# A graph block and a transformer block in one kernel: norm rows spread over slots, wider ranges for projections, modulation in other steps

## The chip, the cores and the metric

The kernel runs on one core of a Trainium2 chip. The metric is the device time of one execution in microseconds (us). Five engines work side by side, each through its own queue of instructions in order: TensorE (PE in the profile) multiplies matrices and transposes, VectorE (DVE) and ScalarE (ACT) work on rows and can read PE's results, GpSimd (POOL) works on rows in SBUF, and SyncE (SP) issues the DMA transfers. They wait for each other by semaphores. All data is float32; a product of two float32 tiles shows as two matmul records in the trace.

## What is computed

Input x has 4 batch elements of 1024 tokens of 512 features; there is one condition vector of 512 features per element. Two blocks follow each other:

```python
# block 0: graph attention; each node looks at 20 nodes, 16 heads, two directions d
self_feat = concat(v, q) @ W_self.T + b_self
for d in range(2):
    aff = einsum(qh, kh) / sqrt(32)            # qh, kh: projections of self_feat
    w = softmax(where(cond > 0, aff, NEG) + label_bias)
    output += einsum(einsum(w, kv), Wout[d]) + bout[d]
x = v + relu(output)

# block 1: conditioned transformer, 16 heads of 64, MLP of 2048
mod = silu(c) @ W_mod + b_mod
sh_msa, sc_msa, g_msa, sh_mlp, sc_mlp, g_mlp = split(mod, 6)
x = x + g_msa * attention(layernorm(x) * (1 + sc_msa) + sh_msa, W_qkv, W_out, b_out)
x = x + g_mlp * (gelu(h @ W1 + b1) @ W2 + b2)  # h: layernorm(x) * (1 + sc_mlp) + sh_mlp
```

## The kernel before

The 4096 tokens are 32 tiles of 128 rows. The program is one long sequence written out by hand; each engine executes its part of it in the order in which the Python code calls the functions. There are three stages.

**Graph attention** is the loop `for s in range(-4, NTA + 2)`. In step s the tiles s-1 to s+4 are at different stations of a pipeline: transposes of x (`g_xT`), the self features (`g_self`), scores (`g_scores`, matmuls of line 643), softmax, weights, output rows to DRAM (`x1d`). One PSUM bank, tag "tr", is shared by the transposes of x and of the features, by the transposes of the norm (`norm_T`) and by the modulation (`g_mod`). `g_modload(r)` loads a quarter of W_mod and `g_mod(r)` multiplies it with silu(c); r = 0 and 1 give shift and scale, r = 2 and 3 the gates, which DVE reads from the bank in line 753. The buffer of the loads holds one quarter. In this stage the first batch element is also normalized: `norm_load(0, k)` loads four tiles, `norm_rows(0, k)` subtracts the mean and multiplies by 1/std, a row of tiles at a time, and `norm_T(0, k, c)` transposes 128 features of the four tiles and applies shift and scale into `hT`.

**Attention** has 4 x 8 x 8 = 256 slots: batch element b, pair of heads gp, query tile t. A slot s consists of a fixed part and of fill. In the fixed part PE makes the scores of two heads into the two "sc" tiles (line 960), DVE takes their maxima (`largest`, line 971), ACT the exponentials (`weights`, line 977), which frees the score tiles for the next slot; ACT scales the first head's weights and GpSimd the second's (`scaled`, line 986). DVE transposes the weights of the slot before in blocks of 32 (`turn`, line 995), the first head's ahead of this slot's maxima and the second's behind them, and after each second slot SP moves them into wT by eight DMAs (line 999).

The fill is a list. `add(lo, hi, units, place, f, *args)` says that f may go into any slot from lo to hi and weighs `units` on PE. A planner puts everything at lo first and then moves pieces to the emptiest slot of their range until nothing gets better. Within a slot, fill runs after the fixed part, by `place`: loads (0), attention times v (1), projections (2), transposes of the norm (3), work of DVE, ACT and GpSimd (4). The pieces that matter here:

- `mm_qk(b, gp, k, n, half, bank)`: half of the sum for q (k = 0) or k (k = 1) of a pair of heads and of half n of the tokens, 1 unit; 8 per pair. It needs `hT` of half n. `mm_v` is the same for v, one tile of tokens each.
- `attend` (line 922), `project` (line 940, whose rows DVE adds into `xr` in line 948).
- norm pieces with times `ld`, `rw`, `tr` relative to `at`, the first slot of the batch element.
- Tiles of PSUM for all of these come from one group "mm" of four banks. `xl`, the rows to be normalized, has four buffers, so that a second `norm_load` waits for the transposes of the first; `hT` has two.

Before slot 256 the fill also holds the first seven products of the **MLP** (`first`, from the function `seven`, in slots NS-6 to NS-1, with NS = 256). They need `mlp_rows` and `mlp_weights`, sums that GpSimd makes (lines 431 to 441). Two of the products start with an opening matmul (line 466) that reads `hT`, which `mlp_rows` also writes. The rest of the MLP follows after the slots and isn't touched.

Of the kernel before, what the change touches and what calls it, by code (L numbers as in the profile page):

```python
# [12 lines left out]
F32 = mybir.dt.float32  # L13
I32 = mybir.dt.int32
AF = mybir.ActivationFunctionType
ALU = mybir.AluOpType
# [3 lines left out]
P = 128  # L20
S = 1024
# [20 lines left out]
def cond_block_kernel(  # L42
# [26 lines left out]
    nc = tc.nc  # L69
# [60 lines left out]
    with ExitStack() as gctx:  # L130
        KC0 = GH * 2 * NG // P
        HF = GH * NG
        gp = gctx.enter_context(tc.tile_pool(name="gp", bufs=1))
# [13 lines left out]
        with ExitStack() as sctx:  # L147
# [69 lines left out]
            for h in range(2):  # L217
                pt = sps.tile([P, FC, P], F32, name="pt", tag="s")
                for c in range(FC):
                    k = h * FC + c  # L220
# [43 lines left out]
            for d in range(2):  # L264
# [19 lines left out]
                v = sp.tile([KV, F], F32, name="vrow", tag="vrow", bufs=2)  # L284
# [59 lines left out]
        VB = 4  # L344
# [3 lines left out]
        def norm_load(st, k):  # L348
            for i in range(k * VB, (k + 1) * VB):
                t = rp.tile([P, F], F32, name="xl", tag="xl", bufs=VB)  # L350
                nc.sync.dma_start(t, NORM[st][0][i])
                xl[st, i] = t

        def norm_rows(st, k):
            _, mv, rs, _, _ = NORM[st]
            for i in range(k * VB, (k + 1) * VB):
                nc.vector.tensor_scalar(
                    xl[st, i], xl[st, i], mv[:, i, 0:1], rs[:, i : i + 1], ALU.subtract, ALU.mult
                )

        def norm_T(st, k, c, bank, on_act=True):

# [33 lines left out]

        def mm_qk(b, gp, k, n, half, bank):

            if half == 0:
                if n == 0:  # L400
                    (qT, kT)[k][b, gp] = qp.tile([P, S], F32, name="qk"[k] + "T", tag="qk"[k] + "T", bufs=2)
                part["qk"] = bank("pqk")
            pt = part["qk"]
            for c in (2 * half, 2 * half + 1):
                nc.tensor.matmul(  # L405
                    pt,
                    lhsT=wqk[b, gp][:, c, k, :],
                    rhs=hT[0, 2 * b + n][:, c, :],
                    start=(c == 0),
                    stop=(c == FC - 1),  # L410
                )
            if half == 1:
                if k == 0:
                    nc.scalar.mul(qT[b, gp][:, n * F : (n + 1) * F], pt, float(D**-0.5))
                else:
                    o = kT[b, gp].rearrange("p (c m k) -> p m k c", c=4, m=NT)
                    nc.scalar.copy(o[:, n * 4 : n * 4 + 4], pt.rearrange("p (m k c) -> p m k c", c=4, k=32))
# [371 lines left out]
        for s in range(-4, NTA + 2):  # L789
            if s == -4:  # L790
                for i in range(5):
                    g_load(i)
            else:
                do(g_load, s + 4)
            if s in (1, 7, 13, 19):
                g_modload(s // 6)
            do(g_scores, s)
            if s == NTA:
                ahead(4)
            do(g_weightsT, s - 1)  # L800
            do(g_soft1, s)
            do(g_startscores, s + 1)
            do(g_xT, s + 3)
            do(g_startattend, s - 1)
            do(g_soft2, s)
            do(g_mask2, s + 2)
            do(g_mask1, s + 3)
            do(g_soft3, s)
            do(g_self, s + 2)
            if s >= NTA - 2:  # L810
                ahead((2, 1, 1, 0)[s - NTA + 2])
            do(g_selfT, s + 1)
            do(g_soft4, s)
            if 0 <= s - 2 < NTA:
                statistics(xs.pop(s - 2), mv1[:, s - 2, :], wp)
            do(g_soft5, s)
            do(g_attend, s - 1)
            do(g_selfout, s + 2)
            do(g_rows, s - 1)
            do(g_start, s + 3)  # L820
            do(g_sum, s + 4)

            if s in (6, 12, 18, 24):
                g_mod(s // 6 - 1)
            if s == 12:
                rstd(rs1, mv1, 0, NT)
            if s in (14, 21):
                norm_load(0, s // 7 - 2)
            if s in (16, 23):
                norm_rows(0, s // 7 - 2)  # L830
            if s in (17, 18, 19, 20, 24, 25, 26, 27):
                norm_T(0, s // 24, (s - 17) % 7, bank_l0)
            if s == 25:
                load_qk(0, 0)
                load_v(0, 0)
                load_qk(0, 1)
                load_v(0, 1)
# [11 lines left out]
    with ExitStack() as actx:  # L849
        ap_ = actx.enter_context(tc.tile_pool(name="ap", bufs=1, reuse_waits="tile"))  # L850
        MM = dict(tag="mm", bufs=4)
        NP = 2 * NGRP
# [9 lines left out]
        def bank(name):  # L862
            return ps.tile([P, F], F32, name=name, **MM)
# [32 lines left out]

        def mm_v(b, g, n):

            if n == 0:
                vt[b, g] = vp.tile([P, NT, GW], F32, name="v", tag="v", bufs=2)  # L900
            if n % 2 == 0:
                part["v"] = ps.tile([P, 2, GW], F32, name="pvv", **MM)
            pt = part["v"]
            for c in range(FC):
                nc.tensor.matmul(  # L905
                    pt[:, n % 2, :],
                    lhsT=hT[0, 2 * b + n // VB][:, c, n % VB * P : (n % VB + 1) * P],
                    rhs=wv[b, g][:, c].rearrange("p k f -> p (k f)"),
                    start=(c == 0),
                    stop=(c == FC - 1),  # L910
                )
            if n % 2 == 1:
                nc.scalar.copy(vt[b, g][:, n - 1 : n + 1, :], pt)
# [90 lines left out]
        def home_q(tag):  # L1004
            return lambda: qp.tile([P, S], F32, name="ex", tag=tag, bufs=2)
# [16 lines left out]
        def add(lo, hi, units, place, f, *args):  # L1022
            fill.append((lo, hi, units, place, lambda: f(*args)))

        for b in range(B):
            s0 = b * NP * NT
            for gp in range(NP):
                g, p = divmod(gp, 2)
                at = s0 + gp * NT
                if gp == 0 and b > 0:  # L1030
                    for h, (ld, rw, tr) in enumerate(((-14, -11, -9), (-7, -6, -5))):
                        add(at + ld, at + ld, 0, 0, norm_load, 0, 2 * b + h)
                        add(at + rw, at + rw, 0, 4, norm_rows, 0, 2 * b + h)
                        for c in range(FC):
                            add(at + tr + c // 2, at + tr + c // 2, 0.4, 3, norm_T, 0, 2 * b + h, c, bank)

                if at > 0:
                    for k in range(2):
                        for n in range(2):
                            for half in range(2):  # L1040
                                add(at - (8 if gp > 0 else 3), at - 2, 1, 2, mm_qk, b, gp, k, n, half, bank)
                if p == 0:
                    for n in range(NT):
                        lo, hi = (at - 12, at + 1) if g > 0 else (max(at - 3, 0), at + 3)
                        add(lo, hi, 1, 2, mm_v, b, g, n)

                for k in range(NB):
                    lo = at + QT * k + LAG
                    add(lo, lo + (lo < NS - 8), 2, 1, attend, b, gp, k)
                if p == 1:  # L1050
                    for n in range(NT):
                        lo = at + QT * (NB - 1) + LAG + (3 if g == 0 else 2)
                        add(lo, lo + (7 if g == NGRP - 1 else 10), 1, 2, project, b, g, n)
                if gp == 0:
                    lo = max(at - 3, 0)
                    add(lo, lo, 0.5, 2, gates_of, b)
                    for n in range(NT):

                        lo = at + (1 + n if b == 0 else 13 + n // 2)
                        add(lo, lo, 0, 0, load_rows, b, n)  # L1060
                        add(lo + 1, lo + 1, 0, 4, gate_rows, b, n)
                if p == 0:
                    add(at + 8, at + 8, 0, 0, load_out, b, g)
                    add(at + 9, at + 9, 0, 4, gate_out, b, g)
                if at - 16 >= 0:
                    add(at - 16, at - 16, 0, 0, load_qk, b, gp)
                if p == 0 and at - 24 >= 0:
                    add(at - 24, at - 24, 0, 0, load_v, b, g)
# [1 line left out]

        add(NS - 20, NS - 20, 0, 4, rstd, rs2, mv2, 0, 3 * NT)
        add(NS - 18, NS - 18, 0, 0, norm_load, 1, 0)
        add(NS - 12, NS - 12, 0, 4, norm_rows, 1, 0)
        for c in range(FC):
            add(NS - 9 + c // 2, NS - 9 + c // 2, 0.4, 3, norm_T, 1, 0, c, bank)
        for i, at in enumerate((NS - 9, NS - 8, NS - 13, NS - 11)):
            add(at, at, 0, 0, load_w1, i, "wqk" if i < 2 else "wv")
        add(NS - 7, NS - 7, 0, 4, mlp_rows)
        for i in range(2):
            add(NS - 6, NS - 6, 0, 4, mlp_weights, nc.gpsimd, i, home_q(("qT", "kT")[i]))  # L1080

        def short():
            return op_.tile([P, F], F32, name="s", tag="s", bufs=2)
# [9 lines left out]

        first = seven(bank, True, short, up_lhs(0), up_rhs, 2, room0, done0)
        for k, f in enumerate(first):
            at = NS - 6 + (0, 1, 2, 2, 3, 4, 5)[k]
            add(at, at, (1.5, 1, 1.5, 1, 1, 1, 1)[k], 2, f)


# [242 lines left out]
```

## Time and profile before

| what | value |
|---|---|
| median of 3 runs | 3222.82 us (3215.42 to 3228.33) |
| the profiled execution | 3225.88 us |
| its span, first to last instruction | 3224.2 us |
| mean granted TensorE clock | 0.988 |
| graph attention, first to last scores (L643) | 99 to 443 us |
| attention slots, first to last scores (L960) | 462 to 2389 us |
| HBM read, written | 109.08 MB, 25.17 MB |

The page shows one execution. Its busy times count an instruction from start to end; the ends of matmuls are modelled, and a matmul that waits within its record counts as busy. "Idle before" is the time for which an engine stood still ahead of an instruction, and the name behind "<-" is what ended it. The granted clock is given in windows; the trace holds the moments at which it changes between 1.0 and 0.5.

### The profile page before, as it was taken

How to read it: one execution, taken by the hardware profiler on the slowest of the kernel's cores; microseconds unless marked ns; L12 is line 12 of the kernel's file. 1: busy time of each engine (PE TensorE's matmuls, PEld its weight loads, DVE VectorE, ACT ScalarE, POOL GpSimd, SP SyncE). 2: the span in 40 equal slices, each digit the busy share in tenths (PEclk: the TensorE clock that was granted, in tenths of full speed). 3: DMA queues.
4: the chain of work that ended last, by engine and by line, in shares of the span. 5: the costliest groups of instructions: out<-in, count | busy, mean ns of one | idle time of the engine just before them, and what ended most of it. 6: DMA issues, size and time to landing. Idle time of an engine off the chain costs nothing.

```text
span 3224.2 us, 39270 instructions
## 1 busy us (share of the span) xinstructions
PE 3165.6 (98%) x14571; PEld 1953.0 (61%) x14571; DVE 1943.2 (60%) x2718; ACT 1406.3 (44%) x2312; POOL 1063.8 (33%) x580
## 2 busy tenths in 40 slices
PE   8999999999999999999999999999999999999999
PEld 6666665544444544445544445544457888888888
DVE  3687766777757777767777767776865332223222
ACT  1344446555555555555555555555641221122111
POOL 1343325444433544333543433544342101110010
PEclk8999999999999999999999999999999999999999
DMA  4223317777766776767776766776772101101010
GB/s 162 79 92 109 100 54 187 159 165 164 175 156 172 178 173 155 172 158 169 183 172 161 162 162 172 183 166 157 177 167 105 40 27 40 39 14 40 27 39 14
DMA packets 272850, 405.29 MB, mean 126 GB/s; under 512 B 24660, under 2 KB 97424, under 8 KB 272660
## 3 DMA queue, kind: packets, MB, share of 16 engines
q1 hardware_dynamic: 272660, 402.78, 50.0%
q8 instruction: 116, 1.90, 0.2%
q14 instruction: 74, 0.61, 0.1%
HBM read 109.08 MB, written 25.17 MB: 42 GB/s over the span
## 4 chain that ended last, share of the span: by engine, by line
PE 84%; DVE 7%; issue 2%; POOL 2%; DMA 2%; ACT 2%; SPq 1%; POOLq 0%; DVEq 0%; ACTq 0%
PE psc L960 14%; PE pqk L405 14%; PE pav L922 12%; PE pvv L905 7%; PE pout L940 6%; PE mbd L454 5%; PE mbu L454 5%; PE mad L454 3%; PE mau L454 3%; PE mcd L454 2%; PE mdd L454 2%; PE mdu L454 2%; PE mcu L454 2%; PE pa L643 1%; PE pf L603 1%
## 5 line engine op out<-in xcount | busy, mean ns | idle before, releaser
L986 POOL TENSOR_SCALAR w<-w,sm 128x1024 f32<-128x1024 f32 x256 | 728.2, 2845 | 1116.5 <-DVE sm L982 1116.5
L977 ACT ACTIVATE w<-psc,mx 128x1024 f32<-128x1024 f32 x512 | 570.2, 1114 | 780.2 <-DVE mx L971 778.3
L971 DVE TENSOR_REDUCE mx<-psc 128x1 f32<-128x1024 f32 x512 | 601.5, 1215 | 293.3 <-PE psc L960 291.9
L995 DVE STREAM_TRANSPOSE wd<-w 128x1024 f32<-128x1024 f32 x512 | 633.9, 1238 | 151.3 <-ACT w L984 133.4
L960 PE MATMUL psc<-kT,qT 64*128 64x512 f32 x2048 | 535.1, 624 | 14.0 <-ACT w L977 12.8
L922 PE MATMUL pav<-wT,v 128*64 128x256 f32 x4096 | 475.3, 384 | 0.8 <-DMA wT<-wd 0.8
L405 PE MATMUL pqk<-hT,wqk 128*128 128x512 f32 x1024 | 472.7, 603 | 0.0
L922 PEld LDWEIGHTS pav<-wT,v 128*64 128x64 f32 x4096 | 286.8, 137 | 229.0 <-issue 81.0
L960 PEld LDWEIGHTS psc<-kT,qT 64*128 64x128 f32 x2048 | 195.2, 188 | 289.9 <-issue 175.8
L405 PEld LDWEIGHTS pqk<-hT,wqk 128*128 128x128 f32 x1024 | 185.7, 190 | 247.3 <-issue 243.7
L984 ACT ACTIVATE w<-w,sm 128x1024 f32<-128x1024 f32 x256 | 291.0, 1137 | 0.0
L940 PE MATMUL pout<-wout,oT 128*128 128x512 f32 x512 | 244.9, 617 | 0.0
L905 PE MATMUL pvv<-wv,hT 128*128 128x256 f32 x1024 | 239.4, 384 | 0.0
L905 PEld LDWEIGHTS pvv<-wv,hT 128*128 128x128 f32 x1024 | 190.4, 190 | 65.9 <-issue 42.8
L438 POOL TENSOR_TENSOR tx<-hT 128x512 f32<-128x512 f32 x8 | 10.2, 1270 | 566.6 <-DVE hT L378 566.6
L940 PEld LDWEIGHTS pout<-wout,oT 128*128 128x128 f32 x512 | 92.5, 193 | 139.1 <-issue 125.9
L643 PE MATMUL pa<-kp,sfT 128*128 128x320 f32 x512 | 145.0, 437 | 1.4 <-ACT sfT L618 1.4
L471 ACT COPY mbu<-mau 128x512 f32<-128x512 f32 x30 | 17.1, 570 | 287.2 <-PE mau L454 287.2
L643 PEld LDWEIGHTS pa<-kp,sfT 128*128 128x128 f32 x512 | 95.7, 192 | 38.1 <-ACT sfT L618 1.9
L603 PE MATMUL pf<-wx,xT 128*128 128x512 f32 x256 | 115.3, 593 | 0.3 <-DVE pf L585 0.3
L948 DVE TENSOR_TENSOR xr<-pout,xr 128x512 f32<-128x512 f32 x128 | 84.6, 676 | 50.0 <-PE pout L940 49.5
L454 PE MATMUL mad<-w,hs 128*128 128x256 f32 x512 | 113.1, 379 | 0.0
(276 smaller groups left out, 3556.0 us busy)
## 6 DMA issues: line engine op xcount, KB each, us to landing
wT<-wd SPq DMA_DIRECT2D x1024, 256.0 KB
wqk<-in_w_qkv SPq DMA_DIRECT2D x64, 256.0 KB
xs<-in_x SPq DMA_DIRECT2D x36, 256.0 KB
x1d<-xs SPq DMA_DIRECT2D x32, 256.0 KB
xl<-x1d SPq DMA_DIRECT2D x32, 256.0 KB
wv<-in_w_qkv SPq DMA_DIRECT2D x32, 256.0 KB
xr<-x1d SPq DMA_DIRECT2D x32, 256.0 KB
wout<-in_w_out SPq DMA_DIRECT2D x16, 512.0 KB
```

The source lines that it names most:

```text
L405: nc.tensor.matmul(pt, lhsT=wqk[b, gp][:, c, k, :], rhs=hT[0, 2 * b + n][:, c, :], start=(c == 0), stop=(c == FC - 1),)
L454: nc.tensor.matmul(t[:, q * HB : (q + 1) * HB], lhsT=lhs(which, q, k), rhs=rhs(which, k), start=(fresh and q == 0 and k == 0), stop=(k == ...
L643: nc.tensor.matmul(pas[i][:, n, :HF], lhsT=sfT2[i][:, c, :], rhs=kp[:, b, c, n * HF : (n + 1) * HF], start=False, stop=(c == FC - 1), skip ...
L905: nc.tensor.matmul(pt[:, n % 2, :], lhsT=hT[0, 2 * b + n // VB][:, c, n % VB * P : (n % VB + 1) * P], rhs=wv[b, g][:, c].rearrange("p k f ...
L922: nc.tensor.matmul(po[j * D : (j + 1) * D, :], lhsT=vt[b, g][:, m, p * P + j * D : p * P + (j + 1) * D], rhs=w[:, j, :, m, :], start=(m == 0),
L940: nc.tensor.matmul(po, lhsT=oT[b, g][:, p, n * P : (n + 1) * P], rhs=wout[b, g][:, p, :], start=(p == 0), stop=(p == 1),)
L960: nc.tensor.matmul(sc[j][:, n * F : (n + 1) * F], lhsT=qT[b, gp][q, t * P : (t + 1) * P], rhs=kT[b, gp][q, n * F : (n + 1) * F], start=Tru ...
L971: nc.vector.tensor_reduce(mx, sc, axis=AX.X, op=ALU.max, negate=True)
L977: nc.scalar.activation(w, sc, AF.Exp, bias=mx, accum_out=sm)
L984: nc.scalar.mul(w, w, sm)
L986: nc.gpsimd.tensor_scalar(w, w, sm, None, ALU.mult)
L995: nc.vector.transpose(wd[j][:, :, at, :], wn.pop((b, gp, t, j)).rearrange("p (m k) -> p m k", k=U))
```

## The change

There are four edits. `norm_rows` is split: `norm_row` does one row of tiles and is called on its own, in graph attention two per step, in the slots one or two per slot. The fill of a change of batch element moves: loads, rows and transposes come earlier, and q, k and v of the new element may start up to 9 slots ahead (first half of the tokens) or 5 slots ahead (second half), instead of 3. As halves of different sums may now interleave, each open sum keeps its own entry in `part`, and the tiles for q, k and v are made by whichever piece comes first. The projections of the last pair of heads must end two slots earlier. In graph attention the last two modulation products move from steps 18 and 24 to 22 and 29, and one load from step 19 to 23. Ahead of the MLP, rows, transposes, loads of W1, GpSimd's weight sums and the seven products move to earlier slots, one product to a slot.

```diff
+        def norm_row(st, i):
+            _, mv, rs, _, _ = NORM[st]
+            nc.vector.tensor_scalar(
+                xl[st, i], xl[st, i], mv[:, i, 0:1], rs[:, i : i + 1], ALU.subtract, ALU.mult
+            )
+
         def norm_rows(st, k):
-            _, mv, rs, _, _ = NORM[st]
             for i in range(k * VB, (k + 1) * VB):
-                nc.vector.tensor_scalar(
-                    xl[st, i], xl[st, i], mv[:, i, 0:1], rs[:, i : i + 1], ALU.subtract, ALU.mult
-                )
+                norm_row(st, i)
...
+            held = (qT, kT)[k]
+            if (b, gp) not in held:
+                held[b, gp] = qp.tile([P, S], F32, name="qk"[k] + "T", tag="qk"[k] + "T", bufs=2)
             if half == 0:
-                if n == 0:
-                    (qT, kT)[k][b, gp] = qp.tile([P, S], F32, name="qk"[k] + "T", tag="qk"[k] + "T", bufs=2)
-                part["qk"] = bank("pqk")
-            pt = part["qk"]
+                part["qk", k, n] = bank("pqk")
+            pt = part["qk", k, n]
...
-            if s in (1, 7, 13, 19):
+            if s in (1, 7, 13, 23):
                 g_modload(s // 6)
...
-            if s in (6, 12, 18, 24):
-                g_mod(s // 6 - 1)
+            if s in (6, 12, 22, 29):
+                g_mod((s - 5) // 6 - s // 29)
...
-            if s in (16, 23):
-                norm_rows(0, s // 7 - 2)
+            if 15 <= s - s // 22 * 7 <= 16:
+                for i in range(2):
+                    norm_row(0, s // 22 * VB + 2 * ((s - 15) % 7) + i)
...
-            if n == 0:
+            if (b, g) not in vt:
                 vt[b, g] = vp.tile([P, NT, GW], F32, name="v", tag="v", bufs=2)
             if n % 2 == 0:
-                part["v"] = ps.tile([P, 2, GW], F32, name="pvv", **MM)
-            pt = part["v"]
+                part["v", n // 2] = ps.tile([P, 2, GW], F32, name="pvv", **MM)
+            pt = part["v", n // 2]
...
-                    for h, (ld, rw, tr) in enumerate(((-14, -11, -9), (-7, -6, -5))):
+                    for h, (ld, rws, tr) in enumerate(
+                        ((-18, (-15, -14, -13, -12), -11), (-10, (-9, -9, -8, -8), -7))
+                    ):
                         add(at + ld, at + ld, 0, 0, norm_load, 0, 2 * b + h)
-                        add(at + rw, at + rw, 0, 4, norm_rows, 0, 2 * b + h)
+                        for n, rw in enumerate(rws):
+                            add(at + rw, at + rw, 0, 4, norm_row, 0, (2 * b + h) * VB + n)
...
-                                add(at - (8 if gp > 0 else 3), at - 2, 1, 2, mm_qk, b, gp, k, n, half, bank)
+
+                                lo = at - (8 if gp > 0 else (9, 5)[n])
+                                add(lo, at - (2 if gp < NP - 1 else 4), 1, 2, mm_qk, b, gp, k, n, half, bank)
                 if p == 0:
                     for n in range(NT):
-                        lo, hi = (at - 12, at + 1) if g > 0 else (max(at - 3, 0), at + 3)
+                        lo, hi = (at - 12, at + 1) if g > 0 else (max(at - (9, 5)[n // VB], 0), at + 3)
                         add(lo, hi, 1, 2, mm_v, b, g, n)
...
-        add(NS - 12, NS - 12, 0, 4, norm_rows, 1, 0)
+        for n in range(VB):
+            add(NS - 15 + n, NS - 15 + n, 0, 4, norm_row, 1, n)
         for c in range(FC):
-            add(NS - 9 + c // 2, NS - 9 + c // 2, 0.4, 3, norm_T, 1, 0, c, bank)
-        for i, at in enumerate((NS - 9, NS - 8, NS - 13, NS - 11)):
+            add(NS - 11 + c // 2, NS - 11 + c // 2, 0.4, 3, norm_T, 1, 0, c, bank)
+        for i, at in enumerate((NS - 14, NS - 11, NS - 13, NS - 12)):
             add(at, at, 0, 0, load_w1, i, "wqk" if i < 2 else "wv")
         add(NS - 7, NS - 7, 0, 4, mlp_rows)
         for i in range(2):
-            add(NS - 6, NS - 6, 0, 4, mlp_weights, nc.gpsimd, i, home_q(("qT", "kT")[i]))
+            add(NS - 9 + i, NS - 9 + i, 0, 4, mlp_weights, nc.gpsimd, i, home_q(("qT", "kT")[i]))
...
-            at = NS - 6 + (0, 1, 2, 2, 3, 4, 5)[k]
+            at = NS - 7 + k
             add(at, at, (1.5, 1, 1.5, 1, 1, 1, 1)[k], 2, f)
```

## The prediction

> **What bounds the kernel now.** I read the page's busy line first, then who TensorE (PE) waited for, then PE's and VectorE's (DVE) timelines at those waits.
>
> ```profile
> PE 3165.6 (98%) x14571; PEld 1953.0 (61%) x14571; DVE 1943.2 (60%) x2718; ACT 1406.3 (44%) x2312; POOL 1063.8 (33%) x580
> ```
> ```profile
> PE psc L960 <- ACT w L977: 12.8, 7, 2.2
> PE ptn L371 <- DVE gates L753: 7.0, 2, 4.2
> ...
> PE mb L466 <- POOL hT L440: 2.0, 1, 2.0
> ```
>
> PE is the bound, and the change alters none of its matmuls, so it can win only PE's waits and what follows them. 98% hides part of that: a matmul after a wait can run slow and count as busy. At the first change of batch element PE's timeline (start, length, idle before) has:
>
> ```profile
> 851.94 2.29 PE L960 MATMUL psc<-kT,qT 64*128 64x512 f32 x8
> 854.16 3.67 PE L922 MATMUL pav<-wT,v 128*64 128x256 f32 x32
> 859.80 4.97 PE L960 MATMUL psc<-kT,qT 64*128 64x512 f32 x8 [1.97 <-ACT w L977]
> 864.70 4.95 PE L940 MATMUL pout<-wout,oT 128*128 128x512 f32 x8
> 870.46 1.99 PE L960 MATMUL psc<-kT,qT 64*128 64x512 f32 x8
> ```
>
> After 1.97 us of idling the scores take 4.97 us instead of 1.99 and two projections 4.95 instead of 3.70. The clock events of the trace grant half speed for 6.83 us from 860.42. DVE meanwhile:
>
> ```profile
> 852.45 1.26 DVE L948 TENSOR_TENSOR xr<-pout,xr 128x512 f32<-128x512 f32 x2
> 853.64 2.60 DVE L357 TENSOR_SCALAR xl<-xl,mv,rs 128x512 f32<-128x512 f32 x4
> 856.17 1.23 DVE L995 STREAM_TRANSPOSE wd<-w 128x1024 f32<-128x1024 f32 x1
> 857.33 2.31 DVE L971 TENSOR_REDUCE mx<-psc 128x1 f32<-128x1024 f32 x2
> ...
> 891.46 2.58 DVE L357 TENSOR_SCALAR xl<-xl,mv,rs 128x512 f32<-128x512 f32 x4 [2.37 <-DMA xl<-x1d]
> ```
>
> Four norm rows stand ahead of the maxima; the exponentials wait for the maxima, the next scores for the exponentials (they free the score banks). The second group of rows also waits 2.37 us for its load.
>
> **A slot table.** A slot runs from one group of score matmuls to the next. PE's work in it, start to start in undisturbed stretches: scores 1.93, attend 3.61, half a q or k projection 1.78, v of one tile 1.80, output projection 1.82, four transposes 0.52. Summed by the planner's slots, this meets the trace within 0.2 us in slots 44 to 69 of the first batch element except in slots 54, 55, 59 and 60: 2.32, 4.05, 2.74 and 2.42 over, 11.5 us. The next two changes have 13.2 and 13.1: **37.8 us** (idle 11.3, half clock 18.8, the rest scores that wait inside their record). Every other slot is PE-bound. DVE's own slot is 4.93 us (two transposes, two maxima, small ones; 856.17 to 861.1), plus 0.63 per projection's row and 0.53 per norm row. A slot with nothing in its way is never under 5.53.
>
> **Part 1, rows one or two to a slot and wider ranges for projections.** Before, slots 52 to 60 have 5.5 to 6.6 us of PE work, because q, k and v of the next element may start only 3 slots ahead, and DVE has 4.93 + 1.26 + 2.60 = 8.8 in slot 53. After, by the planner's rule, PE's work in slots 52 to 62 is 7.36, 6.61, 6.58, 7.35, 7.36, 8.35, 8.36, 7.35, 7.32, 8.37, 9.10, and slots 61 to 67, 9.1 to 10.8 before, come down to 5.5 to 9.1: the sum of slots 36 to 71 is 269.0 both ways. DVE's worst slots are 55 and 56 (4.93 + 0.63 + 1.06 = 6.6, under 7.35), 52 (6.1 under 7.36) and 53 (6.2 under 6.61). So the 37.8 us go, and next late is PE itself. Costs:
> - The second load moves from slot 57 to 54, its rows from 58 to 55. It waits for the last transposes of slot 54 (they read the old rows) and stands on SP behind that slot's eight transfers of wT; behind it are only those of slot 56. In slot 50 before, in the same place behind wT, xl was issued at slot start + 9.96 and landed at +14.2 to +16.2 (semaphore events). That is slot 55 + 7.6; DVE is ready at + 6.4 and waits 1.2 us. Its maxima of slot 56 come 0.7 late, inside that slot's 1.8 of slack (7.36 - 5.53): nothing. If landing takes 7.3 us (as at 884.16 before, behind five weight loads that now come after it), the stall is 2.0 plus up to 3.4 of half clock, three times: 16 us. Below nothing it can't go. I take 1.5 in all, as the nearest row is that of slot 50.
> - k of the first half stays half summed from slot 58 to 62, two v tiles from 63 to 67: they hold up to three of the four "mm" banks. The tightest reuse is slot 69 (second projection at +7.36, its bank freed by ScalarE at about +7.0, after exponentials and scaling) and the gate's two banks in slot 61 (about 0.5 spare). No wait, so nothing; the second rival prices the loss of this cover.
> - The evictions that move with the projections (0.6 to 1.0 us each on ScalarE) land in slots where it has some 2 us free. The moved q, k and v need weights loaded 8 or more slots earlier.
>
> [...] GpSimd scales w (2.84 us) in each slot just as a row would start[...]. The trace: the rows at 853.64 and 854.09 took 0.53 and 0.54 in the middle of GpSimd's 852.63 to 855.52; only the third took 1.25. At +0.72 a slot everything still fits. I go by the rows.
>
> **Part 2, modulation in graph attention.**
>
> ```profile
> 304.60 1.93 PE L744 MATMUL pm<-wm,scT 128*32 128x256 f32 x32
> 309.31 0.66 PE L371 MATMUL ptn<-ident,xl 128*128 128x128 f32 x4 [2.78 <-DVE gates L753]
> ```
> ```profile
> 378.58 0.66 PE L371 MATMUL ptn<-ident,xl 128*128 128x128 f32 x4 [4.19 <-DVE gates L753]
> 379.07 6.16 PE L643 MATMUL pa<-kp,sfT 128*128 128x320 f32 x16
> ```
>
> The norm's transposes come straight after the modulation in the one "tr" bank, and DVE reads that bank behind a step's work. From the starts of L643, a step is 10.28 us, with transposes 10.72, with modulation 1.72 more. Step 18 took 16.23 (3.8 over), 24 took 16.99 (4.55) and 25, at half clock, 12.41 (1.7): **10.0 us**. In steps 22 and 29 the next user of the bank comes after the next step's scores and weight transposes (4.86 us); DVE's read ends 3.0 us into that step (4.75 in an ordinary step, less 1.72 of modulation). Without this cover it would be the old wait. What stays is lateness from the rows (two per step; DVE has 0.3 us free in a step): 0.43 us was lost at 298 so; I keep 0.4. SP's load for the last modulation (two DMAs) moves to step 23 and waits for step 22's matmuls as it did for step 18's; x and adjacency loads behind it run four steps ahead. The gates are first read in attention slot 0, after step 33. **Gain 9.6.**
>
> **Part 3, the way into the MLP.** From slot 244 of 256 (2305.55) to slot 255 (2387.11) the trace takes 81.6; the table, with 1.73 for each of the seven products and 0.86 for each opening matmul, says 71.7 before and after: 9.9 over, 2.05 of it below plus half clock for 3.41 us.
>
> ```profile
> 2355.28 1.93 PE L466 MATMUL mb<-hT,ident 128*128 128x512 f32 x2 [2.05 <-POOL hT L440]
> ```
> ```profile
> 2351.37 1.28 POOL L438 TENSOR_TENSOR tx<-hT 128x512 f32<-128x512 f32 x1
> ```
>
> After, this opening is in slot 249 ahead of GpSimd's sums, one product goes into each slot, and the rows are one to a slot. New waits: product 1 in slot 250 needs the first of GpSimd's sums, ready at slot 249 + 12.7 as in the trace (2352.7 against 2340.00), and PE gets there at 6.34 + 5.54 = 11.9: 0.8. Behind the sums GpSimd scales w of slot 250 about 1 us late, where DVE's transpose waits for it: 0.3. GpSimd's weight sums (8 x 0.7) go into slots 247 and 248, where 2.8 beside its 2.85 just fits the slot. Two projections in slot 247: 0.2. On SP, four w1 DMAs now follow wT of slot 242 and of 244 and two weight loads no longer delay that of 248. Bounds: 0 to 9.9; I take **8.2**.
>
> **Sum.** 37.8 - 1.5 + 9.6 + 8.2 = 54.1 from the profiled execution's 3225.9: 3171.8. Its time lies 3 us over the median of the runs, so 3169 against the median; I say **3171**.
>
> **Price of what is left.** [...] Here 1.44 us at 1382.96 brought half clock for 6.83, and 2.78 at 306.54 brought none. [...] by the trace, up to 5.4. I use the trace.
>
> **Rivals.**
> - **Half stays.** xl lands late in slot 55, or rows and xr chase each other, so that one of the two stalls survives: 37.8/2, and half of part 3: 3172 + 19 + 4 = 3195. For it: the old 2.37 us wait. Against: no weights ahead of the load. 0.10.
> - **Bank starvation (slower).** If a tile in slots 61 to 70 must wait for ScalarE's eviction in its own slot (+7.0 while PE is there at about +5.5), 1.5 idle and 3.4 of half clock follow: 10 x 4.9 x 3 = 147, so 3319. It decides once three held banks meet two short-lived tiles in a slot. For it: margins of 0.3 to 0.5. Against: in no slot do the planner's tiles need that. 0.04.
> - [...]
> - **As summed**, 0.82, with 3161 to 3186 as its own range.
>
> The range reaches to the first rival: 3161 to 3196. Half a per cent (16 us) is about what a measurement of this kernel can tell from no change: faster 0.92, same 0.04, slower 0.04.
>
> **What would show it.** Right: no idle over 1 us before scores L960 between slots 48 and 64, granted clock 1.0 there, a change of element 11 to 13 us shorter, no wait of PE on gates, none on hT L440. Wrong: rows of over 1.5 us, DVE waiting over 3 us on xl, PE waiting on ScalarE's or DVE's eviction before pav, pqk or pvv, new half-clock stretches.

## The result and the profile after

The changed kernel takes 3181.3 us in the median of 4 runs (3172.86 to 3187.09), against 3222.94 of the kernel before (3215.42 to 3228.33): a ratio of 0.987, 95% interval 0.9839 to 0.9901. That is 41.6 us less. The forecast was 3171, with a range of 3161 to 3196. Run again later beside other kernels it took 3175.39 us (3173.84 to 3179.68) against 3224.15, ratio 0.9852, interval 0.9833 to 0.987.

The page of the profiled execution (span 3182.3 us) has this busy line:

```profile
PE 3142.3 (99%) x14571; PEld 1938.9 (61%) x14571; DVE 1941.9 (61%) x2718; ACT 1406.2 (44%) x2312; POOL 1066.0 (33%) x580
```

The work is the same (14571 matmuls), but PE is busy for 23.3 us less, because less of it runs at half clock (mean granted clock 0.993, before 0.988) or waits inside a record (the records of the attention scores sum to 517.1 us, before 535.1). The list of who waited for whom (engine, line, releaser, sum in us, times, longest) has no entry for the gates and none for `hT` from GpSimd any more. Scores behind ScalarE (12.8 us in seven waits before) are down to the last line shown, and one wait is new, the first line shown:

```profile
PE mc L458 <- POOL tx L442: 1.9, 1, 1.9
...
PE psc L965 <- ACT w L982: 0.8, 2, 0.5
```

(Lines moved by up to five: scores are L965, maxima L976, exponentials L982, the norm's transposes L374, its rows L356.)

**Where the time came from.** Each stage is cut at the first matmul of its kind in the trace. "Again" is the profiled execution of the changed kernel's later runs; the cut between the first two rows is the first matmul into `pa`, the score tile of graph attention. The last column is what the forecast said.

| stage (us) | before | after | again | after - before | again - before | forecast |
|---|---|---|---|---|---|---|
| start, up to the first matmul into `pa` | 92.2 | 96.5 | 92.7 | +4.3 | +0.5 | 0 |
| graph attention, up to the first scores of slot 0 | 369.7 | 360.6 | 360.6 | -9.1 | -9.1 | -9.6 |
| three changes of element: slots 36-71, 100-135, 164-199 | 846.6 | 813.5 | 812.4 | -33.1 | -34.3 | -36.3 |
| slots 244-254 | 81.6 | 77.7 | 76.0 | -3.9 | -5.5 | -8.2 |
| the other slots | 997.0 | 997.7 | 997.2 | +0.7 | +0.2 | 0 |
| from slot 255 to the end | 837.1 | 836.3 | 833.8 | -0.8 | -3.3 | 0 |
| sum | 3224.2 | 3182.3 | 3172.7 | -41.9 | -51.4 | -54.1 |

The column "before" is one execution. Stages with half clock differ between executions of the same instructions: in `e_graph` and `e_mlp` below, which leave the three changes as they were, these took 841.0 and 846.7 us. So the gain of 33.1 is known to about 6 us. With the change they repeat better: 813.5, 812.4, and 813.1 in `e_wout`, which does not touch them either.

The first change of batch element, where the old kernel idled for 1.97 us and then ran at half clock for 6.83, on PE's timeline now (start, length, idle before):

```profile
866.18 3.67 PE L927 MATMUL pav<-wT,v 128*64 128x256 f32 x32
869.78 1.98 PE L945 MATMUL pout<-wout,oT 128*128 128x512 f32 x4
872.26 3.17 PE L965 MATMUL psc<-kT,qT 64*128 64x512 f32 x8 [0.49 <-ACT w L982]
```

One trace of lateness is left: an idle time of 0.49 us, and scores that take 3.17 us instead of 1.99. The granted clock stays at 1.00 from 848 to 886 us. DVE's timeline at that place says why:

```profile
862.91 0.67 DVE L953 TENSOR_TENSOR xr<-pout,xr 128x512 f32<-128x512 f32 x1
867.41 0.55 DVE L356 TENSOR_SCALAR xl<-xl,mv,rs 128x512 f32<-128x512 f32 x1 [3.84 <-DMA xl<-x1d]
868.16 0.55 DVE L356 TENSOR_SCALAR xl<-xl,mv,rs 128x512 f32<-128x512 f32 x1 [0.20 <-DMA xl<-x1d]
868.62 1.24 DVE L1000 STREAM_TRANSPOSE wd<-w 128x1024 f32<-128x1024 f32 x1
869.78 2.31 DVE L976 TENSOR_REDUCE mx<-psc 128x1 f32<-128x1024 f32 x2
```

The rows of slot 55 (from 856.98) wait 3.84 us for their load, and slot 56's maxima stand behind them. SP issued this load only behind the eight transfers of wT, 11.3 us after the start of slot 54 (850.43):

```profile
853.09 8.51 SPq L1004 DMA_DIRECT2D wT<-wd  x8
861.70 3.53 SPq L351 DMA_DIRECT2D xl<-x1d  x4
```

In graph attention the modulation is now followed by the next step's scores, and PE has no wait there (before, it stood still for 2.78 and 4.19 us):

```profile
350.98 1.93 PE L748 MATMUL pm<-wm,scT 128*32 128x256 f32 x32
352.84 4.57 PE L647 MATMUL pa<-kp,sfT 128*128 128x320 f32 x16
```

Ahead of the MLP, GpSimd's timeline and then PE's show the new wait:

```profile
2306.97 2.84 POOL L991 TENSOR_SCALAR w<-w,sm 128x1024 f32<-128x1024 f32 x1 [0.33 <-DVE sm L987]
2311.64 2.51 POOL L881 TENSOR_TENSOR wout<-wout,gate 128x512 f32<-128x512 f32 x2 [1.83 <-DMA wout<-in_w_out]
2314.11 1.27 POOL L442 TENSOR_TENSOR tx<-hT 128x512 f32<-128x512 f32 x1
```
```profile
2309.19 4.38 PE L927 MATMUL pav<-wT,v 128*64 128x256 f32 x32
2315.43 2.52 PE L458 MATMUL mc<-tx,ex 128*128 128x256 f32 x8 [1.86 <-POOL tx L442]
2317.88 3.10 PE L965 MATMUL psc<-kT,qT 64*128 64x512 f32 x8
```

GpSimd first waits 1.83 us for the load of `wout`, then multiplies it with the gate for 2.51 us (`gate_out`, which the change did not touch), and only then makes the first sum `tx` that product 1 needs. Before, the multiplication stood in the same place, but there its load had landed and it did not wait:

```profile
2348.91 2.51 POOL L876 TENSOR_TENSOR wout<-wout,gate 128x512 f32<-128x512 f32 x2
```

### The profile page after: what moved, and what is told of

Its sections match the earlier page's. It is cut to its first block, busy times and chain, and to the rows that moved or that the text cites. A ratio compares the mean times of both kernels' runs of the same rounds, so it can differ in the third digit from the quotient of the medians.

```text
span 3182.3 us, 39273 instructions
## 1 busy us (share of the span) xinstructions
PE 3142.3 (99%) x14571; PEld 1938.9 (61%) x14571; DVE 1941.9 (61%) x2718; ACT 1406.2 (44%) x2312; POOL 1066.0 (33%) x580
## 4 chain that ended last, share of the span: by engine, by line
PE 86%; DVE 5%; SPq 2%; DMA 2%; issue 2%; POOL 2%; ACT 1%; POOLq 0%; DVEq 0%; ACTq 0%
PE psc L965 14%; PE pqk L409 14%; PE pav L927 12%; PE pvv L910 7%; PE pout L945 6%; PE mbd L458 5%; PE mbu L458 5%; PE mad L458 3%; PE mau L458 3%; PE pa L647 2%; PE pf L607 2%; PE mcd L458 2%; PE mdd L458 2%; SPq L1004 2%; PE mdu L458 2%
## 5 line engine op out<-in xcount | busy, mean ns | idle before, releaser
L982 ACT ACTIVATE w<-psc,mx 128x1024 f32<-128x1024 f32 x512 | 570.7, 1115 | 769.3 <-DVE mx L976 768.8
L976 DVE TENSOR_REDUCE mx<-psc 128x1 f32<-128x1024 f32 x512 | 601.3, 1215 | 261.9 <-PE psc L965 260.0
L965 PE MATMUL psc<-kT,qT 64*128 64x512 f32 x2048 | 517.1, 616 | 2.0 <-DVE xs L723 0.9
L965 PEld LDWEIGHTS psc<-kT,qT 64*128 64x128 f32 x2048 | 185.8, 186 | 273.7 <-issue 161.1
```

Of the source, the lines that this page charges most:

```text
L965: nc.tensor.matmul(sc[j][:, n * F : (n + 1) * F], lhsT=qT[b, gp][q, t * P : (t + 1) * P], rhs=kT[b, gp][q, n * F : (n + 1) * F], start=Tru ...
L976: nc.vector.tensor_reduce(mx, sc, axis=AX.X, op=ALU.max, negate=True)
L982: nc.scalar.activation(w, sc, AF.Exp, bias=mx, accum_out=sm)
```

## Experiments

The stages are those of the table, each from one profiled execution. Totals are medians of several executions, each against the kernel before beside it.

### One part of the change at a time

Four kernels, each the kernel before with one part.

**Graph attention alone** (`e_graph`: the edits in the steps, nothing in the slots).

```diff
-            if s in (6, 12, 18, 24):
+            if s in (6, 12, 22, 29):
...
-            if s in (16, 23):
-                norm_rows(0, s // 7 - 2)
+            if 15 <= s - s // 22 * 7 <= 16:
```

> The kernel before with the graph attention edits alone (two modulation products and one load in other steps, rows two to a step). Theory: the edits of the three stages are independent, so graph attention gets shorter by what it did with everything changed (362.8 to 353.8, 9.1 us less), the rest stays within 0.5 us of before, and the total is 3214, 9 us under before. Rival, the start: the 4.3 us by which everything ahead of the first scores got longer belongs to a part of the change; then it shows again here (if this part brings it) and the total is only 5 us under before. If it shows in neither this nor the other parts, it is chance of one execution.

Measured: 3216.33 us against 3223.27 (ratio 0.9972, interval 0.996 to 0.9985). Graph attention 361.0 instead of 369.7 us, so 8.7 less; the start 93.1, close to the 92.2 of before. The part stands by itself. It does not bring the longer start.

**The way into the MLP alone** (`e_mlp`: rows, transposes, loads, weight sums and products earlier).

```diff
-        add(NS - 12, NS - 12, 0, 4, norm_rows, 1, 0)
+        for n in range(VB):
+            add(NS - 15 + n, NS - 15 + n, 0, 4, norm_row, 1, n)
...
-            at = NS - 6 + (0, 1, 2, 2, 3, 4, 5)[k]
+            at = NS - 7 + k
```

> The kernel before with the edits ahead of the MLP alone (rows, transposes, loads, weight sums and products earlier; the projections of the last pair keep their old last slot). Theory: slots 244 to 255 get 3 to 5 us shorter (81.6 to about 77.5), as with everything changed (3.9), the first product after GpSimd's sums waits 1.5 to 2 us for them because GpSimd first waits for the load of wout, and half clock follows; total 4 us under before. Rival: these slots lost part of the gain of 8.2 through the other edits (the last pair's projections end two slots earlier); then they get 6 to 8 us shorter here.

Measured: 3217.88 against 3223.27 (ratio 0.9977, interval 0.9968 to 0.9986); slots 244 to 254 took 74.85 us, 6.7 less. That is the rival's number, but not its cause: PE's pieces in each of these slots are the same here as in the changed kernel, and most of the difference lies in the wait and what followed it:

```profile
2355.89 1.99 PE L457 MATMUL mc<-tx,ex 128*128 128x256 f32 x8 [1.44 <-POOL tx L441]
2357.82 1.99 PE L963 MATMUL psc<-kT,qT 64*128 64x512 f32 x8
```

1.44 us and full clock here, 1.86 us and half clock for 3.41 us there. And the old slots differ between executions too: 81.6 us in before, 81.4 in `e_rows`, 83.5 in `e_ranges` and 83.9 in `e_graph`, which do not change them. With 77.7 and 76.0 of the changed kernel, 75.8 and 75.5 of two kernels further down (`e_xl`, `e_late`) and 74.9 here, all with the same pieces in these slots, the part is worth 76.0 against 82.6, so 6.6 us in the mean. The longer start (96.1) appeared here, in a kernel that leaves graph attention alone.

**Spread rows, old ranges** (`e_rows`: loads, rows and transposes in the new slots, q, k and v as late as before) and **wide ranges, rows in one piece** (`e_ranges`: here too loads, rows and transposes come earlier). In both, the projections of the last pair of heads must end two slots earlier, as in the changed kernel.

```diff
 e_rows
-                    for h, (ld, rw, tr) in enumerate(((-14, -11, -9), (-7, -6, -5))):
+                    for h, (ld, rws, tr) in enumerate(
+                        ((-18, (-15, -14, -13, -12), -11), (-10, (-9, -9, -8, -8), -7))
+                    ):
 e_ranges
-                    for h, (ld, rw, tr) in enumerate(((-14, -11, -9), (-7, -6, -5))):
+                    for h, (ld, rw, tr) in enumerate(((-18, -12, -11), (-10, -8, -7))):
...
-                                add(at - (8 if gp > 0 else 3), at - 2, 1, 2, mm_qk, b, gp, k, n, half, bank)
+                                lo = at - (8 if gp > 0 else (9, 5)[n])
...
```

> The kernel before with loads, rows and transposes of the changes of batch element in their new slots, but q, k and v starting 3 slots ahead as before. Theory (a stall is what DVE has in a slot beyond PE's work in it): before, DVE has 8.8 us in slot 53 against 5.6 of PE. Here slot 53 has 6.2 against 6.6, but slot 55 has 7.2 against 5.6 and slot 56 6.0 against 5.5, and xl comes late for slot 55: 2 to 4 us lost per change plus up to 3.4 of half clock, so the three changes gain 15 to 27 of the 33 us that the whole change gained there. Rival 1, the rows in one piece are the cause whatever PE has: gain 31 or more. Rival 2, PE's short slots are the cause whatever the rows: gain under 8.

> The kernel before with the wider ranges for q, k and v and the earlier loads and transposes, but the rows four to a slot (in slots 52 and 56). Theory (DVE's surplus over PE's work in a slot): the two row slots have 7.7 us of DVE against 7.36 of PE, so 0.3 us each is lost, and xl has a slot more to land than with everything changed: the three changes gain 31 to 37 us, no less than the whole change (33), so the spreading of rows brings nothing by itself. Rival 1, rows in one piece stall whatever PE has (2 us of maxima late, then half clock): gain under 20.

Measured: `e_rows` 3211.61 us (ratio 0.9966, interval 0.9951 to 0.9981), the three changes 20.2 us shorter; `e_ranges` 3199.18 (0.9916, 0.9894 to 0.9938), the three changes 33.8 shorter, 0.7 more than with the whole change. The 20.2 come from the fastest of nine executions (3200.91 us); in the median all of `e_rows` is worth 11.7 us, with 15.8 as the most that the interval allows, so 20.2 is more than it usually brings and the expected 15 to 27 is not confirmed. What `e_rows` lacks is PE work in slots 55 to 57. Its PE timeline in slot 56 and after:

```profile
865.02 2.16 PE L963 MATMUL psc<-kT,qT 64*128 64x512 f32 x8
867.11 3.69 PE L925 MATMUL pav<-wT,v 128*64 128x256 f32 x32
873.47 4.52 PE L963 MATMUL psc<-kT,qT 64*128 64x512 f32 x8 [2.67 <-ACT w L980]
```

With 5.5 us of PE work in the slot there is nothing to bridge DVE's rows and their wait for the load (1.25 and 0.66 us), and half clock follows (granted clock 0.94 from 858 to 886 us). In `e_ranges` the first four rows, in one piece, make the maxima of slot 53 late, and the scores of slot 54 wait inside their record:

```profile
858.85 2.30 DVE L356 TENSOR_SCALAR xl<-xl,mv,rs 128x512 f32<-128x512 f32 x4
864.71 3.17 PE L964 MATMUL psc<-kT,qT 64*128 64x512 f32 x8
```

This costs 1.3 us per change (270.95 against 269.62 in `e_late` below, which differs at the changes only in that it spreads these four rows); the second four cost nothing. So what a slot loses is what DVE has in it beyond PE's work. The two kernels' gains (20.2 and 33.8) do not add up to the whole (33.1), and the ranges carry more: with rows spread, wide ranges bring about 13 us; with wide ranges, spreading as the change does it brings nothing. Neither kernel shows one edit alone, since both also start loads, rows and transposes earlier; what the earlier start brings without either was not run.

### The two waits that were left

These kernels are the changed kernel with one edit more, or two. `e_xl`, `e_wout` and `e_both` ran beside the changed kernel itself, `e_late` and `e_best` later, beside the kernel before.

> The changed kernel once more, beside the three below on one chip. Theory: the stages repeat (changes of batch element 271.0 to 271.4 us, graph attention 353.8, slots 244 to 255 77.7 within 3), and what differs between executions is the time up to the first scores, which was 92.1 to 100.2 us in six executions of kernels that do not differ there. Rival: the start belongs to the change, then it is 96 to 97 again.

Measured: the column "again" of the table. Stages between the start and slot 255 repeat within 1.7 us; the start is 92.7 this time, so the rival falls.

**The load ahead of wT** (`e_xl`): all four groups of transposes of the first half (one group for each 128 features) in one slot, the second load behind them.

```diff
-                        ((-18, (-15, -14, -13, -12), -11), (-10, (-9, -9, -8, -8), -7))
+                        ((-18, (-15, -14, -13, -12), -11), (-11, (-9, -9, -8, -8), -7))
...
-                        add(at + ld, at + ld, 0, 0, norm_load, 0, 2 * b + h)
+                        add(at + ld, at + ld, 0, 9 * h, norm_load, 0, 2 * b + h)
...
-                            add(at + tr + c // 2, at + tr + c // 2, 0.4, 3, norm_T, 0, 2 * b + h, c, bank)
+                            add(at + tr + c // 2 * h, at + tr + c // 2 * h, 0.4, 3, norm_T, 0, 2 * b + h, c, bank)
```

> The changed kernel, but all four transposes of the first half in the first of their two slots, and the second load behind them in that slot, ahead of wT of the next slot on SP. Theory: slots 56 and 57 (1.6 us over PE's work per change) are late because the load stands behind wT on SP and DVE waits 3 to 4 us for it; now it lands some 6 us earlier, the wait goes, and each change gets 1 to 1.6 us shorter (271.2 to about 269.9), 3 to 5 us in all. Rival: DVE has too much in slots 55 and 56 anyway (two rows, one output row, transposes and maxima); then the wait goes but the 1.6 us stay, and the total is that of the changed kernel.

Measured: 3176.98 us. The wait for the load is gone and so are the losses of slots 56 and 57, but the changes are 270.9 us, as before the edit. The total is the rival's, but neither cause holds: the loss moved to slot 53. PE's timeline there:

```profile
842.27 3.70 PE L945 MATMUL pout<-wout,oT 128*128 128x512 f32 x8
845.80 1.04 PE L374 MATMUL ptn<-ident,xl 128*128 128x128 f32 x8
847.66 1.25 PE L374 MATMUL ptn<-ident,xl 128*128 128x128 f32 x8 [0.82 <-DVE xr L953]
```

Two projections and four groups of transposes want six "mm" banks in a slot that has four; the third group waits 0.82 us until DVE has read a projection. That is the mechanism of the forecast's second rival, brought about by the experiment. The planner also moved a projection (from slot 57 to 54) and half a q or k (from 62 to 57) in answer to the edit.

**The load of wout earlier** (`e_wout`), and both edits (`e_both`).

```diff
-                    add(at + 8, at + 8, 0, 0, load_out, b, g)
-                    add(at + 9, at + 9, 0, 4, gate_out, b, g)
+                    early = 5 if b == B - 1 and g == NGRP - 1 else 0
+                    add(at + 8 - early, at + 8 - early, 0, 0, load_out, b, g)
+                    add(at + 9 - early * 3 // 5, at + 9 - early * 3 // 5, 0, 4, gate_out, b, g)
```

> The changed kernel with the last load of wout five slots earlier and GpSimd's gate on it three slots earlier (slot 246). Theory: GpSimd's sums for the MLP wait behind that gate, and the gate for its load; with both gone ahead, tx is ready about 3.9 us earlier (1.8 of waiting and most of 2.5 of gating), product 1 does not wait (1.9 before), no half clock follows, slots 250 and 251 get 3 to 4 us shorter. Rival 1: GpSimd then scales w late in slots 246 and 247, DVE's transposes wait and the gain is under 1. Rival 2: tx is late for its own length (hT, the transposes), and the wait stays over 1 us.

> Both of the last two in one kernel. Theory: they lie in different slots, so the gains add: 6 to 9 us under the changed kernel on the same chip, about 3173. Rival: the start differs between executions by more than either gain, and the difference can be seen in the stages only.

Measured: `e_wout` 3177.84, slots 244 to 254 in 74.2 us, 1.8 under the changed kernel beside it and 3.5 under its first profile; `e_both` 3175.87, 73.65. The wait of product 1 is gone. GpSimd's timeline and PE's of `e_wout`:

```profile
2302.20 2.85 POOL L991 TENSOR_SCALAR w<-w,sm 128x1024 f32<-128x1024 f32 x1 [0.35 <-DVE sm L987]
2305.01 1.27 POOL L442 TENSOR_TENSOR tx<-hT 128x512 f32<-128x512 f32 x1
```
```profile
2305.23 3.64 PE L927 MATMUL pav<-wT,v 128*64 128x256 f32 x30 [0.17 <-issue]
2308.80 1.99 PE L458 MATMUL mc<-tx,ex 128*128 128x256 f32 x8
```

`tx` now comes straight behind the scaling. By stages `e_both` is 2.1 us under the changed kernel beside it (2.4 less in these slots, 0.3 more at the changes), so the expected 6 to 9 did not come. By their medians the four kernels measured here cannot be told apart; that is what the rival of `e_both` said. After slot 255 the same instructions took 833.4 to 839.4 us in them.

**The second half's rows one slot later** (`e_late`), and this with the earlier `wout` (`e_best`). PE's order is that of the changed kernel.

```diff
-                        ((-18, (-15, -14, -13, -12), -11), (-10, (-9, -9, -8, -8), -7))
+                        ((-18, (-15, -14, -13, -12), -11), (-10, (-8, -8, -8, -8), -7))
```

> The changed kernel with all four rows of the second half in slot 56 instead of two in 55 and two in 56; TensorE's order is the same. Theory (with e_xl in view): slots 56 and 57 lose 1 to 1.6 us per change because rows in slot 55 wait for a load that stands behind wT; in slot 56 it has landed, and DVE's 7.7 us there stand against 7.4 of PE, so what is left is 0.3 or less: each change 269.9 to 270.2 us instead of 270.7 to 271.4, 1.5 to 4 us in all. Rival: four rows in one piece are late by themselves (maxima of slot 56 2 us later), the scores of slot 57 wait and the change gets longer than 271.4, with half clock in places.

> The changed kernel with the rows as in e_late and wout as in e_wout. Theory: changes of batch element 269.9 to 270.2 each, slots 244 to 255 73.6 to 74.2; by stages 4 to 9 us under the changed kernel, median 3167 to 3172. Rival: the start (92.1 or 96 us) and half clock behind slot 255 (832 to 839 us for the same instructions) differ by as much, and the medians of the two can't be told apart.

Measured: `e_late` 3176.0 us against 3222.46 (ratio 0.986, interval 0.9842 to 0.9878). Each of the three changes takes 269.62 us, a little less than expected, and no slot from 36 to 71 loses over 0.3 us. DVE's row in slot 56 no longer waits:

```profile
871.62 2.30 DVE L356 TENSOR_SCALAR xl<-xl,mv,rs 128x512 f32<-128x512 f32 x4
```

`e_best`: 3172.29 against 3222.46 (0.9842, 0.9824 to 0.986), changes of 269.6 to 269.8 us, slots 244 to 254 in 73.64. By stages it is 5.7 us under the changed kernel's second execution; the medians (3172.3 and 3175.4, not measured side by side) do not separate them.

## Why the prediction was right, and where it was off

- **What bounds it**: right. PE's waits and the half clock behind them were what could be won, and PE is busy for 99% now.
- **37.8 us in the three changes**: right to the tenth against the execution from which it was read. With nothing late (`e_late`) they take 808.9 us, 37.8 under it, and each change had lost what the table said (11.5, 13.2, 13.1). Against the 841.0 us of `e_graph` it would be 32.
- **"I take 1.5 in all" for the second load**: this term was mis-sized; it measured 4.7 us (37.8 - 33.1), and 3.5 in the second execution. DVE was ready at slot 55 + 6.6, as said (+ 6.4). But the load was issued 11.3 us after slot 54's start, not 9.96, because wT's transfers began 2.7 us into slot 54 and 0.6 into slot 50; and its first tile landed 5.7 us after issue, not 4.2. So DVE waited 3.84 us, not 1.2, and slot 56's 1.8 us of slack did not hold it. That is over the 3 us that the forecast named as a sign of being wrong, and the first change got 9.8 us shorter and not 11 to 13 (the others 11.6 and 11.7). `e_late` takes the wait away without moving the load, and the loss goes. The upper bound (up to 3.4 us of half clock each) did not come about.
- **The slot table for DVE**: right in form, but it gave the spreading a worth that it does not have. For the first half of the tokens it saves 1.3 us per change (`e_ranges` against `e_late`); for the second half it puts two rows ahead of their load and costs 1.1 to 1.8 (`e_late` against the changed kernel).
- **Banks, "no wait, so nothing"**: right; PE waited nowhere for an eviction at the changes. `e_xl` shows how near the bound is: with two more groups of transposes in slot 53 each change takes 1.25 us more than in `e_late`.
- **Rows beside GpSimd's scaling**: going by the rows was right in size, but the scaling is not without effect on them. Of the 64 rows of the changed kernel 22 overlap GpSimd's scaling of 2.84 us. Twelve began first and took 0.53 us. Ten began while the scaling ran: six ended within it (three took 0.53 us, three 0.98); the four that were still at work at its end (0.93 to 0.94 us) all ended 0.28 us after it. In before a row took up to 1.41 us. What makes such a row longer no run shows.
- **Graph attention, 9.6**: measured 9.1, and 8.7 alone. The waits of 2.78 and 4.19 us are gone. The allowance of 0.4 for rows was about right (two steps took 10.88 and 10.85 us instead of 10.72); the term that was too small is the modulation, which takes 2.06 us of its step in the new places (12.34 instead of 10.28), not 1.72, twice.
- **The way into the MLP, 8.2**: measured 3.9 and 5.5. The costs that the sum names (0.8, 0.3, 0.2) would leave 8.6. The step that failed is "product 1 in slot 250 needs the first of GpSimd's sums, ready at slot 249 + 12.7 as in the trace". In the changed kernel it was ready at + 14.5, and PE waited 1.86 us (2.00 the second time) where 0.8 was allowed. The multiplication by the gate stands ahead of the sums in both kernels; what is new is its wait of 1.83 us (1.69) for `wout`, whose load SP issued 5.4 us (4.5) after slot 249's start and, before, 3.0. I had taken the interval of one execution of before (12.7, the shortest of four; the longest is 13.8) and did not follow what GpSimd's queue itself would wait for. In the first execution half clock for 3.41 us came on top. Without that wait (`e_wout`, `e_both`, `e_best`) slots 244 to 254 take 73.6 to 74.2 us, 7.4 to 7.9 under before and 8.4 to 9.0 under the mean of the four executions with the old slots (82.6), so the rest of the sum was sound.
- **The start, not in the prediction**: 4.3 us of the first profiled execution's loss are no part of the change (see the last section). That the median still fell into the range owes something to its width: the terms above were too high by 3.2, 0.5 and 4.3 us, all on one side.
- **Rivals**: half stays (3195) and bank starvation (3319) both stayed out. The nearest was the first: its mechanism, a late load in slot 55, is what happened, at a quarter of its price.

## What to carry to other kernels

Spreading work over slots helps only up to the time its input is there: move the consumer behind the landing that the trace shows, and work out the issue of a load from the queue it stands in, since the transfers ahead of it move with the change. For an instruction that is to wait on another engine, write down everything in that engine's queue ahead of the releaser, with what each of those waits for in turn. If single executions differ in a stage that the change doesn't touch, compare stages and not totals before a small gain or loss is explained, and look at several executions of a stage that has half clock in it.

## What the runs showed of the hardware

**Half clock near the start.** All twelve profiled programs do the same up to the first matmul into `pa`, which comes at 92.1 to 93.1, 96.1 to 96.5, or 99.8 to 100.2 us. The clock events grant half speed for 17.07 us from 24.16 in before, and for 23.89 us from 23.00 in the changed kernel's first execution. Windows of PE (busy and records, granted clock, DMA share, GB/s) for before, after and `e_ranges`:

```profile
24.00:60.00 36.00, 36.00 (x174) 0.76 0.30 95
```
```profile
24.00:60.00 36.00, 36.00 (x149) 0.68 0.27 87
```
```profile
24.00:60.00 36.00, 36.00 (x136) 0.58 0.27 87
```

In the same window `e_rows` has the 0.76 of before and `e_best` the 0.58 of `e_ranges`. What decides between them no run shows. The MLP shows the like: from slot 255 on the same instructions took 832.3 to 839.4 us, with 18.8 us of half clock in the 837.1 of before and 15.6 in the 836.3 of the changed kernel.

**Half clock behind a wait.** Between the first matmul into `pa` and slot 255 before has eleven waits of PE of over 1 us. Behind eight of them half clock begins within 1.7 us of the wait's end: for 3.41 us behind 2.05, 2.17 and 4.19, for 6.83 us behind five of 1.44 to 1.97. Behind the other three (1.51, 1.78 and 2.78) none follows. In front of product 1 the changed kernel's first wait (1.86 us) is followed by half clock for 3.41 us from 2316.75; behind the second (2.00 us) the granted clock is 1.00 from 2306 to 2330, and behind the 1.44 us of `e_mlp` product and scores take 1.99 us each. So the length of a wait did not tell, in these executions, whether half clock followed. Nor did it need such a wait: of the half clock in the MLP, three stretches in before and three in the changed kernel have at most 0.72 us of idle PE in the 7 us ahead of them, and why stays open. A leftover wait of 2 us thus cost 2.0 us in one place and, as an estimate, 5.4 in another (in before 1.97 us, and half of 6.83 us at half clock), and the same code can pay either.
